# A gated, quantised feed-forward kernel: other orders in its first slots, and its last output tile in two halves

## The chip, the cores and the metric

The kernel runs on one core of a Trainium2 chip. Time is device microseconds of one execution of the whole program; the table below has the runs of the kernel before. The profile is one further execution, recorded by the hardware profiler.

## The reference

Four sequences of 1024 tokens (x is 4 x 1024 x 512) go through a normalised, gated feed-forward layer whose second half is quantised. Cut to what matters:

```python
scale = cond @ norm_w.T + 1.0
ms = jnp.mean(x * x, axis=-1, keepdims=True)
h = x * (scale[:, None, :] * jax.lax.rsqrt(ms + EPS))
u = h @ up_w.T                                  # up_w: 4096 x 512
val, gate = jnp.split(u, 2, axis=-1)
h = val * jax.nn.gelu(gate, approximate=False)  # 2048 wide
hq = act_quant(h)      # per token: round(h * 127 / max|h|), scaled back
wq = weight_quant(down_w)   # round(w / mean|w|) clipped to -1..1, scaled back
y = hq @ wq.T + x                               # down_w: 512 x 2048
```

## The kernel before

The four sequences are the batches b = 0 to 3. The up projection runs in 16 slots j per batch: slot j makes 128 rows of gate and the same 128 rows of value, for all 1024 tokens, which are two halves h of 512 tokens. float32 operands are split into a high and a low float16 part, and the products of high with high, high with low and low with high are summed in PSUM. Batches 1 to 3 multiply with seven combinations of blocks per slot (`slot`, `product`). Batch 0 instead uses plain products (`plain_half`), and beside them it prepares the weights for everybody: weight tile j is loaded (`w_load`), its largest magnitude is found and turned into a power of two (`w_range`), it is scaled (`w_scale`), turned on TensorE into PSUM (`w_turn`), copied as the high part (`w_high`, ScalarE) and subtracted for the low part (`w_low`, VectorE). A float32 copy goes to SBUF (`w_evac`, ScalarE), GpSimd makes sums of its blocks (`s_sums`), and these too are split and spilled to DRAM for the later batches (`s_all`).

The schedule is written out by hand: every engine runs its own instructions in the order of the program text, and an instruction that waits holds up what stands behind it on the same engine. The SP queue issues nearly all DMAs, in the same manner. PSUM has eight banks, given out by tag: "po" has three, "A" and "E" have two each, "B" has one. Each tag goes round its banks in order of allocation, and a new tile waits for the last reader of the tile that had its bank.

The start, lines 695 to 813, is a chain of its own. x's first 512 tokens are four tiles of 128 tokens (`first_load`, one DMA each, L707). ScalarE sums their squares (`first_sum`, L718); `rsqrt_start` makes one over the root (ScalarE L725, VectorE L726 to L730); the tiles are scaled (`first_scale`, L735 on ScalarE, L737 elsewhere), turned on TensorE into four PSUM banks, one for each block k of 128 columns (`first_turn`, L742), and written to SBUF as the high part (`first_high`, ScalarE L746) and the low part (`first_low`, VectorE L750), both with the batch's column scale, which `cond_undo` brings (VectorE L212 to L215). A few matmuls on zeros (`keep_warm`, L758) run in between. W0's gate half (t = 1) goes the same way ahead of its value half. After that `plain_first` runs slot 0's first half (L533), with `second_part` after 6 and `second_slot` after 16 of its matmuls; `plain_half(1, 0, third_slot)` and `plain_half(2, 0, other_half)` follow.

The scale of batches 1 to 3 is a small piece of work beside all this: products and sums (L178, L179), a turn `cond_over` (L192), the largest and its power of two on VectorE (`cond_range`, L198 to L202), and a matmul that spreads it over the partitions (`cond_spread`, L208), which stands in slot 3.

The down projection of a batch runs among the slots of the next one; that of the last batch stands at the end. There its tiles of 128 tokens and 512 columns (four for each half h) take 16 matmuls each (`down_mm`, L684). VectorE multiplies by the token's scale and adds x (`down_end`, L691), and a DMA stores the tile (L692).

Of the kernel before, what the change touches and what calls it, by code (L numbers as in the profile page):

```python
# [17 lines left out]
P = 128  # L18
# [23 lines left out]
def glu_quant_kernel(  # L42
# [15 lines left out]
    HALF = D // 2  # L58
# [180 lines left out]
    def wn(j):  # L239
        return H[:, W_SLOT[j % 3]]  # L240
# [7 lines left out]
    def w_load(j, ts=(1, 0)):  # L248
        for t in ts:
            SP.dma_start(out=wn(j)[:, t], in_=up_v[j][:, t])  # L250

    def w_range(j, t0=0, t1=2):
        t = slice(t0, t1)
        am = sm.tile([P, 2], F32, name=f"wam_{j}_{t0}", tag="wam")[:, t]
        DVE.tensor_reduce(am, wn(j)[:, t], AX.X, ALU.max, apply_absolute_value=True)
        pow2_floor(am)
        DVE.tensor_scalar(sw[:, j, t], am, 2.0**-100, 1.0 / W_UP, ALU.max, ALU.mult)
        if j not in iv:
            iv[j] = sm.tile([P, 2], F32, name=f"iv_{j}", tag="iv", bufs=3)
        DVE.reciprocal(iv[j][:, t], sw[:, j, t])  # L260

    def w_gain(j):
        DVE.tensor_scalar(sg0[:, j, :], sw[:, j, :], dx[:, 0:1], None, ALU.mult)

    def w_scale(j, ts=(1, 0), eng=POOL):
        for t in ts:
            w, r = wn(j)[:, t], iv[j][:, t : t + 1]
            if eng is ACT:
                ACT.activation(w, w, AF.Copy, scale=r)
            else:  # L270
                eng.tensor_scalar(w, w, r, 1.0, ALU.mult, ALU.mult)
# [16 lines left out]
    def w_high(j, ts=(1, 0)):  # L288
        gate, a21, a22 = a_parts(j)
        g, v = (p.rearrange("p (n f) -> p n f", n=2) for p in pw[j])  # L290
        if 1 in ts:
            ACT.copy(gate[:, :, 0], g)
        if 0 in ts:
            ACT.copy(a21[:, 0], v[:, 0])
            ACT.copy(a22[:, 0], v[:, 1])
# [10 lines left out]
    def w_evac(j):  # L306
        for n in range(2):
            ACT.copy(wf(j)[:, 2 * n : 2 * n + 2].rearrange("p n f -> p (n f)"), pw[j][n])  # L308
# [200 lines left out]
        pass  # L509

    def plain_half(j, h, between=nothing):
        pg = bank("A", 2, name=f"pg_{j}_{h}") if h else bank("B", 1, name=f"pg_{j}_{h}")
        plain(j, 1, h, pg)
        t1 = wpool.tile([P, TOK], F32, name=f"g_{j}_{h}", tag="t1")
        ACT.activation(t1, pg, AF.Gelu, scale=gain(j, 1))
        between()
        pv = bank("E", 2, name=f"pv_{j}_{h}")
        plain(j, 0, h, pv)
        DVE.scalar_tensor_tensor(h_half(j, h), pv, gain(j, 0), t1, ALU.mult, ALU.mult)

    def plain_first(between):

        ps = {1: bank("B", 1, name="pg_0_0"), 0: bank("A", 2, name="pv_0_0")}
        gate, a21, a22 = a_parts(0)
        order = [(1, w, 0, k) for k in range(NK) for w in range(2)]
        order += [(0, w, 0, k) for w in range(2) for k in range(NK)]
        order += [(t, 0, 1, k) for t in (1, 0) for k in range(NK)]
        for n, (t, w, l, k) in enumerate(order):
            if n in between:
                between[n]()  # L530
            a = [gate[:, 0], gate[:, 1]] if t else [a21, a22]
            a = a[k // 2].rearrange("p w (k f) -> p w k f", k=2)
            PE.matmul(  # L533
                ps[t], a[:, w, k % 2, :], XP[:, l, k, :TOK],
                start=w + l + k == 0, stop=l == 1 and k == NK - 1,
            )
        t1 = wpool.tile([P, TOK], F32, name="g_0_0", tag="t1")
        ACT.activation(t1, ps[1], AF.Gelu, scale=gain(0, 1))  # L538
        DVE.scalar_tensor_tensor(h_half(0, 0), ps[0], gain(0, 0), t1, ALU.mult, ALU.mult)
# [132 lines left out]
    def rows_of(b, h, a):  # L672
        r = b * S + h * TOK + a * P
        return slice(r, r + P)
# [3 lines left out]
        SP.dma_start(out=xr, in_=xf[rows_of(b, h, a), :])  # L678
        return xr

    def down_mm(b, h, a, po, js):
        q = q_view(b)
        for j in js:
            PE.matmul(  # L684
                po, q[:, h, j, a * P : (a + 1) * P], wd[:, j, :],
                start=j == 0, stop=j == NJ - 1,
            )

    def down_end(b, h, a, po, xr, dq):
        n = h * NA + a  # L690
        DVE.scalar_tensor_tensor(xr, po, dq[:, n : n + 1], xr, ALU.mult, ALU.add)  # L691
        SP.dma_start(out=of[rows_of(b, h, a), :], in_=xr)  # L692


    ctx.enter_context(tc.manual_schedule())
# [10 lines left out]
    def first_load(n, m=1):  # L706
        SP.dma_start(  # L707
            out=X0[:, n : n + m],
            in_=xf[n * P : (n + m) * P, :].rearrange("(s p) d -> p s d", p=P),
        )  # L710
# [21 lines left out]
    def first_scale(n, eng):  # L732
        r = rs0[:, n : n + 1]
        if eng is ACT:
            ACT.activation(X0[:, n], X0[:, n], AF.Copy, scale=r)  # L735
        else:
            eng.tensor_scalar(X0[:, n], X0[:, n], r, 1.0, ALU.mult, ALU.mult)  # L737

    def first_turn(n, pts):
        for k in range(NK):  # L740
            c = (n % NA) * P
            PE.transpose(pts[k][:, c : c + P], X0[:, n, k * P : (k + 1) * P], ident)  # L742

    def first_high(h, k, pt):
        c = slice(h * TOK, (h + 1) * TOK)
        ACT.activation(XP[:, 0, k, c], pt, AF.Copy, scale=scT[:, k, 0:1])  # L746
# [7 lines left out]
    def keep_warm(n):  # L754

        pz = bank("A", 2, name="pz")
        for i in range(n):
            PE.matmul(pz, warm[:, :P], warm, start=True, stop=True)  # L758

    for n in range(NA):  # L760
        first_load(n)
    w_load(0)
    w_load(1)
    first_load(4, 2)
# [9 lines left out]
        first_sum(n)  # L774
    keep_warm(2)
    pd = cond_spread(cond_range(pm, 0, 1), 0, 1, "A")
    keep_warm(5)
    rsqrt_start(ssq0[:, 0:NA], rs0[:, 0:NA])
    for n in (0, 1, 2):
        first_scale(n, ACT)  # L780
    first_scale(3, DVE)
    w_range(0, 1, 2)
    cond_undo(pd, 0, 1)
    w_scale(0, (1,), DVE)
    ptx = [po_bank(f"ptx_0_{k}") for k in range(3)] + [bank("A", 2, name="ptx_0_3")]
    for n in (0, 3, 1):
        first_turn(n, ptx)
    w_turn(0, [bank("E", 2, name=f"pw_0_{t}") for t in (1, 0)], (1,))
    first_turn(2, ptx)
    w_high(0, (1,))  # L790
    first_high(0, 0, ptx[0])
    w_range(0, 0, 1)
    w_low(0, (1,))
    w_scale(0, (0,))
# [10 lines left out]
    def second_part():  # L805
        w_turn(0, ts=(0,))
        w_high(0, (0,))
        w_low(0, (0,))
        w_scale(1, (1,), ACT)
        for k in range(1, NK):  # L810
            first_low(0, k, ptx[k])
        w_evac(0)
        ACT.activation(start_t, neghalf[:, 0:1], AF.Gelu)  # L813


# [77 lines left out]
    def second_slot():  # L893
        w_turn(1)
        w_high(1)
        w_range(2)
        w_gain(2)
        w_scale(2)
        w_low(1)

    def third_slot():
        w_turn(2)
        w_high(2)
        w_evac(2)
        w_low(2)
        first_scale(4, ACT)
        first_scale(5, DVE)
        first_scale(6, ACT)
        first_scale(7, DVE)
# [13 lines left out]

    plain_first({6: second_part, 16: second_slot})
    w_load(3)
    w_evac(1)
    first_sum(4)
    first_sum(5)
# [24 lines left out]
    w_high(3)  # L953
    w_evac(3)
    w_low(3)
    plain_half(1, 1)
    w_load(6)
    for n in D_LOAD[2]:
        d_load(n)
    w_range(5)  # L960
    w_gain(5)
    w_scale(5)
    s_all(2)
    s_sums(3)
# [4 lines left out]
    w_evac(4)  # L969
    w_low(4)  # L970
    plain_half(2, 1)
    pm = cond_over(mx, 1, B, "po")
    dg = cond_range(pm, 1, B)
    s_all(3)
    for n in D_SUM[2]:
        d_sum(n)
# [255 lines left out]
    for h in range(2):  # L1232
        bring_dq = token_undo(b, dq, h, h + 1)
        if h == 0:
            pos = [bank(t, 1 if t == "B" else 2, name=f"po_end_0_{n}") for n, t in enumerate("ABEA")]
        else:
            pos = [po_bank(f"po_end_1_{a}") for a in range(3)] + [bank("E", 2, name="po_end_1_3")]
        cut = NJ - 4
        for j in range(0, cut, 2):
            for a in range(NA):  # L1240
                down_mm(b, h, a, pos[a], (j, j + 1))
            for f in work[:4]:
                f()
            del work[:4]
        for f in work:
            f()
        work = []
        bring_dq()
        for a in range(NA):
            down_mm(b, h, a, pos[a], range(cut, NJ))  # L1250
            down_end(b, h, a, pos[a], XR[:, h * NA + a], dq)
# [1 line left out]
_INS = ["x", "cond_256", "L0_cond_norm_w", "L0_cond_up_w", "L0_cond_down_w"]  # L1253
_OUTS = [((4, 1024, 512), "float32")]
# [23 lines left out]
```

## Time and profile before

| | |
|---|---|
| median of the runs | 750.74 us (750.51 to 751.12, 3 runs) |
| the profiled execution's own time | 748.98 us |
| its span, first to last instruction | 747.0 us |
| TensorE (PE) busy | 737.6 us, 99% |
| VectorE (DVE) busy | 548.7 us, 73% |
| ScalarE (ACT) busy | 376.7 us, 50% |
| GpSimd (POOL) busy | 199.7 us, 27% |
| granted TensorE clock | 1.000 |
| first matmul of slot 0 (L533) | 13.79 us |
| first matmul of slot 1 (L491) | 21.40 us |

Times within the profile are microseconds from the span's start. In the timeline and the chain, a row gives the start, the length, the engine with its line, the operation, the tile written and the tiles read, and how many instructions are merged. In a row of waits, the two times are the total and the longest. A busy matmul in the profile is not the array's own time: matmuls overlap, and back to back those of 512 columns start 0.216 us apart.

### The profile page before, as it was taken

The numbers are of one execution on the slowest core, as the hardware profiler recorded it, in microseconds if no ns is written. First come the engines' busy times: TensorE is split into PE (matmuls) and PEld (weight loads), VectorE is DVE, ScalarE is ACT, GpSimd is POOL, SyncE is SP. The second block draws the span as 40 slices with busy tenths as digits, with TensorE's granted clock in tenths as the row PEclk, the third lists the DMA queues.
The fourth block names the chain that finished last, engine by engine and source line by source line (L and its number), as shares of the span: only waits on it lengthen the run. The fifth ranks groups of instructions, "written<-read, shape, count | busy, mean of one in ns | idle before, by whom it ended". The sixth has DMA issues, their size and how long they took to land.

```text
span 747.0 us, 9574 instructions
## 1 busy us (share of the span) xinstructions
PE 737.6 (99%) x3481; PEld 343.1 (46%) x3481; DVE 548.7 (73%) x794; ACT 376.7 (50%) x617; POOL 199.7 (27%) x219
## 2 busy tenths in 40 slices
PE   7999999999999999999999999999999999999998
PEld 3554545544444444444444444444444444444443
DVE  7868698897989885536689885454778887445896
ACT  6767456565235664534334656453433665332274
POOL 0499487899010030341010030333020000000200
PEclk9999999999999999999999999999999999999999
DMA  7189739777623433765722424466833333233243
GB/s 250 57 321 177 241 108 261 211 180 172 183 86 111 144 107 105 200 209 146 215 99 98 127 77 169 149 196 163 200 103 105 113 112 106 101 99 112 85 156 112
DMA packets 94250, 111.48 MB, mean 149 GB/s; under 512 B 61430, under 2 KB 62071, under 8 KB 94204
## 3 DMA queue, kind: packets, MB, share of 16 engines
q1 hardware_dynamic: 94058, 110.68, 50.4%
q8 instruction: 27, 0.44, 0.2%
q10 hardware_dynamic: 146, 0.20, 0.1%
q14 instruction: 19, 0.16, 0.1%
HBM read 74.66 MB, written 23.09 MB: 131 GB/s over the span
## 4 chain that ended last, share of the span: by engine, by line
PE 96%; DVE 1%; ACT 1%; DMA 1%; issue 0%; SPq 0%; ACTq 0%; DVEq 0%
PE A L476 33%; PE E L476 16%; PE po L684 11%; PE pg L491 11%; PE pv L491 10%; PE B L476 8%; PE po_end L684 4%; PE pw L279 2%; DMA H<-in_x_dram 1%; DVE gm L603 0%; PE ptx L742 0%; PE pg L533 0%; ACT R L718 0%; ACT L813 0%; ACT H L308 0%
## 5 line engine op out<-in xcount | busy, mean ns | idle before, releaser
L476 PEld LDWEIGHTS <-SXY 128*128 128x128 f16 x2016 | 197.1, 98 | 238.2 <-DMA SXY<-s_dram 0.9
L476 PE MATMUL A<-R,SXY 128*128 128x512 f16 x1152 | 264.8, 379 | 0.0
L476 PE MATMUL E<-R,SXY 128*128 128x512 f16 x576 | 140.0, 379 | 0.0
L570 DVE SCALAR_TENSOR_TENSOR H<-A,sg,t 128x512 f32<-128x512 f32 x48 | 36.0, 750 | 80.9 <-PE A L476 80.9
L581 ACT ACTIVATE t<-t,sg 128x512 f32<-128x512 f32 x48 | 34.6, 720 | 106.5 <-DVE t L580 106.5
L684 PE MATMUL po<-wd,R 128*128 128x512 bf16 x384 | 85.3, 379 | 0.0
L684 PEld LDWEIGHTS <-R 128*128 128x128 bf16 x512 | 50.1, 98 | 60.4
L658 DVE TENSOR_TENSOR H<-H,am 128x1024 f32<-128x1024 f32 x64 | 76.2, 1216 | 0.0
L619 POOL PARTITION_ALL_REDUCE am<-R x8 | 14.5, 1818 | 220.6 <-DVE R L605 220.6
L603 DVE TENSOR_REDUCE gm<-H 128x512 f32<-128x1024 f32 x56 | 69.0, 1232 | 2.9 <-DMA wd<-tn 1.9
L476 PE MATMUL B<-R,SXY 128*128 128x512 f16 x288 | 70.0, 379 | 0.0
L580 DVE TENSOR_TENSOR t<-E,t 128x512 f32<-128x512 f32 x48 | 32.6, 679 | 49.4 <-PE E L476 49.4
L385 POOL TENSOR_TENSOR rs<-ssq,neghalf 128x2 f32<-128x2 f32 (+1 forms) x13 | 9.6, 737 | 205.9 <-DVE ssq L384 205.8
L491 PE MATMUL pv<-R 128*128 128x512 f16 x246 | 61.6, 379 | 0.0
L491 PE MATMUL pg<-R,SXY 128*128 128x512 f16 x252 | 57.8, 379 | 0.5 <-ACT g L538 0.5
L491 PEld LDWEIGHTS <-SXY 128*128 128x128 f16 x378 | 37.0, 98 | 42.9 <-issue 0.7
L491 PEld LDWEIGHTS <-R 128*128 128x128 f16 x366 | 35.8, 98 | 41.8
L567 ACT ACTIVATE t<-B,sg 128x512 f32<-128x512 f32 x48 | 33.0, 687 | 37.2 <-PE B L476 37.2
L666 ACT ACTIVATE H<-H 128x1024 f32<-128x1024 f32 x39 | 40.9, 1048 | 20.8 <-DVE H L658 20.8
L551 ACT COPY t<-A 128x512 f32<-128x512 f32 x48 | 28.0, 583 | 45.1 <-PE A L476 44.7
L562 ACT COPY v<-E 128x512 f32<-128x512 f32 x48 | 28.1, 585 | 32.1 <-PE E L476 29.3
L558 ACT COPY B<-A 128x512 f32<-128x512 f32 x48 | 27.4, 571 | 31.0 <-PE A L476 30.2
(154 smaller groups left out, 905.1 us busy)
## 6 DMA issues: line engine op xcount, KB each, us to landing
SXY<-s_dram SPq DMA_DIRECT2D x48, 640.0 KB, 4.1
SXY<-s_dram SPq DMA_DIRECT2D x48, 256.0 KB, 4.5
s_dram<-SXY SPq DMA_DIRECT2D x11, 896.0 KB, 4.0
H<-in_L_cond_up_w_dram SPq DMA_DIRECT2D x32, 256.0 KB, 3.8
xr<-in_x_dram SPq DMA_DIRECT2D x19, 256.0 KB, 5.0
out_dram<-xr SPq DMA_DIRECT2D x19, 256.0 KB, 2.3
s_dram<-R SPq DMA_DIRECT2D x5, 896.0 KB, 12.8
R<-in_L_cond_down_w_dram SPq DMA_DIRECT2D x8, 512.0 KB, 6.0
```

Source lines behind the costliest of these rows:

```text
L476: PE.matmul(o, s[:, w, k, :], tv[:, :, c, l, k, :], start=start and n == 0, stop=stop and n == len(TERMS) - 1, skip_group_check=True,)
L491: PE.matmul(ps, a[k // 2][:, w, k % 2, :], XP[:, l, k, h * TOK : (h + 1) * TOK], start=n == 0, stop=n == len(terms) - 1,)
L551: ACT.copy(cur["t2"], cur["A"])
L562: ACT.copy(cur["v"], cur["E"])
L567: ACT.activation(cur["t1"], pb, AF.Gelu, scale=gain(g, 1))
L570: DVE.scalar_tensor_tensor(h_half(g - 1, 0), prev["A"], gain(g - 1, 0), prev["t1"], ALU.mult, ALU.mult)
L580: DVE.tensor_tensor(prev["t2"], prev["E"], prev["t2"], ALU.add)
L581: ACT.activation(prev["t2"], prev["t2"], AF.Gelu, scale=gain(g - 1, 1))
L603: DVE.tensor_reduce(gm[0], v, AX.X, ALU.max, apply_absolute_value=True)
L658: DVE.tensor_tensor(v, v, r.to_broadcast([P, 2, TOK]), ALU.mult)
L666: ACT.activation(v, v, AF.Copy, bias=MAGIC)
L684: PE.matmul(po, q[:, h, j, a * P : (a + 1) * P], wd[:, j, :], start=j == 0, stop=j == NJ - 1,)
```

## The change

Seven things are changed, and the arithmetic stays as it is:

1. x's first four tiles come in two DMAs of two tiles instead of four of one.
2. `w_range` is cut in two, `w_largest` and `w_factor`. At the start, W0's largest (gate half) stands ahead of the root of x, and the rest of the range stays behind the scalings.
3. Tile 3 of x is scaled by VectorE, 0 and 1 by ScalarE, 2 by GpSimd; W0's gate half is scaled by GpSimd instead of VectorE, ahead of `cond_undo`. TensorE turns the tiles in the order 3, 0, 2, 1 and then W0. The first block's `first_high` stands ahead of `w_high(0)`. Seven warm-up matmuls stand where five did.
4. In `plain_first`, the first four matmuls go through both of the first two blocks with the high part before the low part.
5. In slots 0 to 2: `w_evac(0)` goes from `second_part` (ahead of the table load for GELU) to after `plain_first`; the gate of slot 1's first half gets a bank of tag A instead of B; `w_low(1)` for the gate stands ahead of `w_range(2)`; `w_low(2)` ahead of `w_evac(2)`.
6. `cond_over` and `cond_range` for batches 1 to 3 go from after `plain_half(2, 1)` to before and after `plain_half(1, 1)`.
7. The last tile's 512 columns are done as two halves of 256 in two PSUM banks, the second after everything else; its store is issued from ScalarE's queue.

```diff
+    def w_largest(j, t0=0, t1=2):
         t = slice(t0, t1)
         am = sm.tile([P, 2], F32, name=f"wam_{j}_{t0}", tag="wam")[:, t]
         DVE.tensor_reduce(am, wn(j)[:, t], AX.X, ALU.max, apply_absolute_value=True)
+        return am
+
+    def w_factor(j, am, t0=0, t1=2):
+        t = slice(t0, t1)
         pow2_floor(am)
...
+    def w_range(j, t0=0, t1=2):
+        w_factor(j, w_largest(j, t0, t1), t0, t1)
...
-        pg = bank("A", 2, name=f"pg_{j}_{h}") if h else bank("B", 1, name=f"pg_{j}_{h}")
+        pg = bank(*(("A", 2) if h or j == 1 else ("B", 1)), name=f"pg_{j}_{h}")
...
-        order = [(1, w, 0, k) for k in range(NK) for w in range(2)]
+        order = [(1, w, 0, k) for w in range(2) for k in range(2)]
+        order += [(1, w, 0, k) for k in range(2, NK) for w in range(2)]
...
-    def down_mm(b, h, a, po, js):
+    def down_mm(b, h, a, po, js, c=slice(None)):
...
-                po, q[:, h, j, a * P : (a + 1) * P], wd[:, j, :],
+                po, q[:, h, j, a * P : (a + 1) * P], wd[:, j, c],
...
-        SP.dma_start(out=of[rows_of(b, h, a), :], in_=xr)
+        eng.dma_start(out=of[rows_of(b, h, a), c], in_=xr)
...
-    for n in range(NA):
-        first_load(n)
+    first_load(0, 2)
+    first_load(2, 2)
...
-    keep_warm(5)
+    keep_warm(7)
+    am = w_largest(0, 1, 2)
     rsqrt_start(ssq0[:, 0:NA], rs0[:, 0:NA])
-    for n in (0, 1, 2):
-        first_scale(n, ACT)
-    first_scale(3, DVE)
-    w_range(0, 1, 2)
+    for n, eng in ((3, DVE), (0, ACT), (2, POOL), (1, ACT)):
+        first_scale(n, eng)
+    w_factor(0, am, 1, 2)
+    w_scale(0, (1,))
     cond_undo(pd, 0, 1)
-    w_scale(0, (1,), DVE)
...
-    for n in (0, 3, 1):
+    for n in (3, 0, 2, 1):
         first_turn(n, ptx)
     w_turn(0, [bank("E", 2, name=f"pw_0_{t}") for t in (1, 0)], (1,))
-    first_turn(2, ptx)
+    first_high(0, 0, ptx[0])
     w_high(0, (1,))
-    first_high(0, 0, ptx[0])
...
-        w_evac(0)
         ACT.activation(start_t, neghalf[:, 0:1], AF.Gelu)
...
         w_turn(1)
         w_high(1)
+        w_low(1, (1,))
         w_range(2)
         w_gain(2)
         w_scale(2)
-        w_low(1)
+        w_low(1, (0,))
...
         w_high(2)
+        w_low(2)
         w_evac(2)
-        w_low(2)
...
     w_load(3)
+    w_evac(0)
     w_evac(1)
...
     w_low(3)
+    pm = cond_over(mx, 1, B, "po")
     plain_half(1, 1)
...
     w_gain(5)
+    dg = cond_range(pm, 1, B)
     w_scale(5)
...
     plain_half(2, 1)
-    pm = cond_over(mx, 1, B, "po")
-    dg = cond_range(pm, 1, B)
...
+        cols = [slice(0, D)] * (NA - 1) + [slice(0, HALF if h else D)]
...
-            down_mm(b, h, a, pos[a], range(cut, NJ))
-            down_end(b, h, a, pos[a], XR[:, h * NA + a], dq)
+            c, xr = cols[a], XR[:, h * NA + a]
+            down_mm(b, h, a, pos[a][:, c], range(cut, NJ), c)
+            down_end(b, h, a, pos[a][:, c], xr[:, c], dq, c)
+    c = slice(HALF, D)
+    po = bank("B", 1, name="po_end")[:, c]
+    down_mm(b, h, a, po, range(NJ), c)
+    down_end(b, h, a, po, xr[:, c], dq, c, ACT)
```

More of the change, by code (lines that the diff above doesn't have):

```diff
@@ L250, in w_load @@
             SP.dma_start(out=wn(j)[:, t], in_=up_v[j][:, t])
-    def w_range(j, t0=0, t1=2):
+    def w_largest(j, t0=0, t1=2):
         t = slice(t0, t1)
@@ L684, in down_mm, with down_end @@
             PE.matmul(
-                po, q[:, h, j, a * P : (a + 1) * P], wd[:, j, :],
+                po, q[:, h, j, a * P : (a + 1) * P], wd[:, j, c],
                 start=j == 0, stop=j == NJ - 1,
             )
-    def down_end(b, h, a, po, xr, dq):
+    def down_end(b, h, a, po, xr, dq, c=slice(None), eng=SP):
         n = h * NA + a
         DVE.scalar_tensor_tensor(xr, po, dq[:, n : n + 1], xr, ALU.mult, ALU.add)
-        SP.dma_start(out=of[rows_of(b, h, a), :], in_=xr)
+        eng.dma_start(out=of[rows_of(b, h, a), c], in_=xr)
     ctx.enter_context(tc.manual_schedule())
@@ L1240, in glu_quant_kernel @@
             for a in range(NA):
-                down_mm(b, h, a, pos[a], (j, j + 1))
+                down_mm(b, h, a, pos[a][:, cols[a]], (j, j + 1), cols[a])
             for f in work[:4]:
```

## The prediction

> **What bounds the kernel now.** I read the page first, then TensorE's waits, the start of the chain, and the timelines of three stretches: the first 32 us, 44 to 60 us, and the end.
>
> ```profile
> PE 737.6 (99%) x3481; PEld 343.1 (46%) x3481; DVE 548.7 (73%) x794; ACT 376.7 (50%) x617; POOL 199.7 (27%) x219
> PE 96%; DVE 1%; ACT 1%; DMA 1%; issue 0%; SPq 0%; ACTq 0%; DVEq 0%
> ```
>
> TensorE is busy in 99% of the span and carries 96% of the chain. So only holes in TensorE's row can be won, and a hole is worth its own length. All of TensorE's waits:
>
> ```profile
> PE ptx L742 <- ACT H L735: 1.6, 1, 1.6
> PE pz L758 <- DVE eps L698: 1.4, 1, 1.4
> PE pd L208 <- DVE dg L202: 1.1, 2, 0.6
> PE pg L533 <- ACT R L746: 0.8, 1, 0.8
> PE pg L491 <- ACT g L538: 0.5, 1, 0.5
> PE pw L279 <- DVE H L271: 0.2, 1, 0.2
> ```
>
> The same view from 58 us on is empty. The change can only move the first 58 us and the 3.6 us after the last matmul. The chain of the first stretch (start, length):
>
> ```profile
> 1.77 4.30 DMA H<-in_x_dram
> ...
> 6.10 1.35 ACT R L718 x4
> ...
> 17.27 0.96 ACT H L308 x2
> ...
> 18.24 1.28 ACT L813
> ...
> 20.76 0.60 ACT g L538
> ...
> 21.40 2.75 PE pg L491 x12
> ```
>
> x's second tile lands at 6.07; ScalarE's squares, VectorE's root and the scalings follow; then evacuation (L308), table load (L813) and GELU (L538) hold the matmuls of slot 1 until 21.40.
>
> **The change, part by part.** Two anchors: R is when x's root is ready (9.35 before), W is when w_high(0) has written W0's gate half (13.14 before, L292 at 12.56 + 0.58).
>
> *x in pairs: +0.66.* Before, the squares start at 4.14, 6.10, 6.77 and 7.42; after x1's landing three are left, at a pitch of 0.66. A pair lands whole. If the first pair lands when x1 did, four are left, and R is one square later. The second pair, due when x3 was (7.42 is when SP, waiting for x3, issued again), comes just in time for the third. Bounds: the windows moved 288, 271 and 307 GB/s from 2 to 5 us, so norm_w and two tiles (0.78 MB) could be in by 4.7, and R 0.55 earlier; at worst the pair lands with x3 and R is 2.0 later. I take +0.66, from the row of x1. SP issues two DMAs fewer, so W0's leave 0.96 sooner, but the DMA engines' share is 0.83 to 1.07 from 2 to 13 us: issue is not their limit, nothing.
>
> *W0's largest ahead of the root: 0.* The reduce (0.68) now waits for W0's gate half, and behind it on VectorE stands the root, for which every scaling waits. The half is next in line after x3, one 0.66 later, so about 8.08; the reduce ends at 8.79. ScalarE's square root would end at 9.14. Cover: 0.35; without it the reduce counts in full from there.
>
> *Scalings, turns, W0: W is 0.30 nearer to R.* Before, W = R + 3.79: ScalarE scaled three tiles until R + 1.98, and VectorE scaled W0 at R + 1.99. After: tile 3 (VectorE, 0.49) at R + 0.52, tiles 0 and 1 (ScalarE, pitch 0.62) at R + 0.71 and R + 1.33, tile 2 on GpSimd, which had nothing to do before 13.10. TensorE turns 3, 0, 2, 1 at 0.43 each from R + 0.56, so the last tile's first block is done at R + 2.1; first_high(0) R + 2.13 to 2.76. W0 on GpSimd (0.69 against 0.48) R + 1.4 to 2.1, its turn R + 2.3 to 2.9, w_high then ends at R + 3.48. [...]
>
> ```profile
> 27.77 1.34 DVE L737 TENSOR_SCALAR H<-H,rs 128x512 f32<-128x512 f32 x2
> ...
> 56.30 0.14 DVE L199 TENSOR_SCALAR d<-d 3x1 f32<-3x1 f32 x1
> ...
> 56.65 0.95 DVE L202 TENSOR_SCALAR dg<-ident,d 3x3 f32<-3x3 f32 x1
> ...
> 55.93 2.28 POOL L327 TENSOR_TENSOR SXY<-H,SXY 128x768 f16<-128x768 f32 x2
> ```
>
> Beside GpSimd two scalings take 1.34 instead of 2 x 0.49, and a 3x3 takes 0.95 instead of 0.2; but the 3x1 one takes its 0.14. [...] By the row, one-column operations pass, and only tile 3 and tile 2 exclude each other. VectorE issues next in line, GpSimd 0.09 to 0.12 after a semaphore (13.10 after 12.98), so VectorE should go first: tile 2 is then ready at R + 1.2, before TensorE wants it at R + 1.4. If GpSimd goes first, tile 3 comes at R + 1.1, all turns slip, and W is R + 4.05 (+0.26). I take -0.30.
>
> *From W to slot 1: -0.93.* VectorE goes without a hole from w_low(0) through w_range(1) and the four first_low to 19.42, which is W + 6.28; w_low(0)'s second part waited 0.17 for ScalarE, which is now ahead, so W + 6.13. Before, slot 1's matmuls began at W + 8.26 since GELU stood behind evacuation (1.07) and table load and held bank B. Now evacuation comes after, and the gate half of slot 1 has bank A. The last first_low then decides: matmul of block 3 at W + 6.25, four more of 0.216, slot 1 at W + 7.33. The halved order (both k before the low parts) gives first_high's second block its 0.6 and costs nothing. Evacuation of W0 now ends at W + 8.4 and is wanted at W + 10.7; GELU of slot 1 and w_high(2) come 3.4 and 4.6 after slot 1's start instead of 2.9 and 4.0, wanted at 6.05. w_low(1)'s gate part, put ahead of w_range(2), makes w_scale(2) end 0.3 before its turn: the thinnest cover, priced at what it lacks. Bounds -0.6 (the hole alone) to -1.0.
>
> *The spread of the other batches' scale: -0.74, and a new wait: +0.48.* Before, TensorE's slots end at 56.95 and the spread waits to 57.7 for dg. Moved two slots up, dg is made about 50 us, where VectorE idles 4.7 us: free. But pm takes one of the three "po" banks two turns earlier. w_turn(4) now gets both banks of w_turn(3), not one old bank and the first of them.
>
> ```profile
> 46.01 0.41 DVE L304 TENSOR_TENSOR SXY<-pw,SXY 128x256 f16<-128x256 f32 x1
> ...
> 45.61 1.04 PE L279 MATMUL pw<-ident,H 128*128 128x128 f32 x8
> ```
>
> Their last reader ends at 46.43, the turn's second half began at 46.04: with the semaphore's 0.1, 0.48 late. Both engines hang on the same earlier matmuls, so the lag travels. Bounds: 0 to +0.8. pm itself also waits for mx (40.34, wanted 40.43): a cover of 0.05.
>
> *The last tile in halves: -0.45.*
>
> ```profile
> 742.49 1.61 DVE L691 SCALAR_TENSOR_TENSOR R<-po_end,dq_end,R 128x512 f32<-128x512 f32 x2
> ...
> 743.27 1.20 SPq L692 DMA_DIRECT2D out_dram<-R  x2
> ```
>
> The final operation (0.74) falls to 256 columns, 0.27 less (128x256 against 128x512 from PSUM is 0.41 against 0.69). Its 128 KB, not 256 KB, at some 400 GB/s (the window at 10 us) is up to 0.32 shorter; I take 0.25, as rows of 1 KB appear nowhere. Added: 32 short matmuls for 16, +0.04 at half of 0.216 (if loads don't hide, up to +0.7; but turns pair a 141 ns load with a matmul every 0.108), and ACT's issue 0.37 against 0.33 (ScalarE's own work is over at 736.7, so nothing stands ahead of it). Bounds -0.1 to -0.6.
>
> Sum: +0.66 - 0.30 - 0.93 - 0.74 + 0.48 - 0.45 = **-1.28 us**. The profiled execution took 748.98 (span 747.0 and 1.98 around it), so 747.7; its time is 1.76 below the median of the runs, 750.74, from which the same step gives **749.5**.
>
> **The rivals.** What a measurement of this kernel can tell from no change is about 0.2%, 1.5 us.
>
> *The pair lands by its bytes.* For: x1 came 1.4 us later than the bytes moved would allow, so one late packet may have set 6.07. Against: the squares behind it follow with no room. Then R is between +0.27 (W0's half at 8.08 and its reduce now decide) and -0.55: 748.2 to 749.1.
>
> [...]
>
> [...]
>
> **How the numbers follow.** The sum as it stands 0.45 (its own range 748.6 to 750.2), the early pair 0.25, the port 0.18, the clock or a like loss 0.12. Under 749.24 lie the early pair (0.25) and two fifths of the first case (0.17): 0.42. Over 752.24 lie half of the last case, where the loss of 1.7 meets a pair that lands with x3 (0.06), and a little for what isn't listed: 0.08. The rest, 0.50. The range of eight in ten is 747.9 to 751.2.
>
> **What would show it.** Right: the first square at about 6.1, tile 2 on GpSimd after tile 3 on VectorE, slot 1's matmuls near 20.8, TensorE's wait for GELU gone, a hole of about 0.5 in w_turn(4) near 45, none at the spread, and the last VectorE operation at 0.47. Wrong: squares that start before 5.5, small VectorE operations stretched beside GpSimd, matmuls every 0.43 after 10 us, or any wait of TensorE after 58 us.

## The result, and the profile after

| | before | after |
|---|---|---|
| median of 15 runs each, on the same chip | 750.45 us | 748.08 us |
| lowest to highest | 748.99 to 751.61 | 747.37 to 750.33 |
| the profiled execution | 748.98 (span 747.0) | 747.51 (span 745.7) |

The ratio is 0.9974 (95% interval 0.9965 to 0.9983), which is 1.95 us less (1.3 to 2.6): faster, and by more than the 0.2% that can be told from no change. The profiled pair moved by 1.47 us and its spans by 1.3. The prediction had 1.28 for that pair.

In what follows, line numbers are those of the changed kernel, which stand 7 or 8 higher in the helpers (L742 is now L750). From the page, TensorE's row among the engines, and the chain's shares:

```profile
PE 737.4 (99%) x3481; PEld 344.7 (46%) x3499; DVE 548.7 (74%) x794; ACT 376.5 (50%) x616; POOL 201.6 (27%) x221
PE 98%; DMA 1%; ACT 0%; issue 0%; DVE 0%; SPq 0%
```

TensorE works as long as before (737.6), and its share of the chain rose from 96 to 98%. So what was won are holes and the tail, as the prediction had it. All of TensorE's waits after the change (total, times, longest):

```profile
PE ptx L750 <- DVE wam L136: 1.8, 1, 1.8
PE pz L766 <- DVE eps L706: 1.4, 1, 1.4
PE pg L541 <- ACT SXY L299: 0.7, 1, 0.7
PE pg L541 <- ACT R L754: 0.2, 1, 0.2
```

Three lines of before are gone: the waits for the scale's spread (1.1; of it 0.6 at 57 us, the rest near 7 us, where nothing depended on it), the wait of slot 1 for GELU (0.5), and 0.2 ahead of W0's turn (L279). The first wait names the one-column L136; L136 starts at 10.66, and what the turn needs is tile 3's scaling, which began at 10.26 just ahead of it on VectorE. The chain from the start to slot 1 (start, length):

```profile
1.77 5.89 DMA H<-in_x_dram
...
8.22 0.81 ACT R L726 x3
...
10.26 0.49 DVE H L745
...
10.82 1.95 PE ptx L750 x16
12.76 0.45 PE pw L286 x4
13.24 0.39 ACT SXY L299
...
13.72 0.70 ACT R L754
...
20.35 0.86 PE pv L541 x4
21.21 2.59 PE pg L498 x12
```

The DMA at its head is now the second pair, until 7.66. Evacuation, table load and GELU, which ended the chain of before ahead of slot 1, are not in it any more; TensorE's own matmuls run on from slot 0 into slot 1. A row of the chain begins where the row before it ends; the timelines of ScalarE and TensorE have the starts themselves, of w_high(0) and of slot 1:

```profile
13.24 0.59 ACT L299 CAST SXY<-pw 128x512 f16<-128x512 f32 x1
...
21.05 2.75 PE L498 MATMUL pg<-R,SXY 128*128 128x512 f16 x12
```

The squares on ScalarE and the start of VectorE's and GpSimd's work, from the three engines' timelines:

```profile
5.71 0.63 ACT L726 ACTIVATE R<-H 128x512 f32<-128x512 f32 x1 [2.94 <-DMA H<-in_x_dram]
...
7.68 0.63 ACT L726 ACTIVATE R<-H 128x512 f32<-128x512 f32 x1 [0.64 <-DMA H<-in_x_dram]
```

```profile
8.36 0.69 DVE L255 TENSOR_REDUCE wam<-H 128x1 f32<-128x512 f32 x1 [1.39 <-DMA H<-in_L_cond_up_w_dram]
9.38 0.17 DVE L734 TENSOR_SCALAR ssq<-ssq 128x4 f32<-128x4 f32 x1 [0.34 <-ACT newton L733]
...
10.26 0.49 DVE L745 TENSOR_SCALAR H<-H,rs 128x512 f32<-128x512 f32 x1
10.66 0.15 DVE L136 TENSOR_SCALAR wam<-wam 128x1 int32<-128x1 int32 x1
```

```profile
10.40 0.91 POOL L745 TENSOR_SCALAR H<-H,rs 128x512 f32<-128x512 f32 x1 [9.98 <-DVE rs L738]
```

The third square waits for the second pair. W0's largest (L255) ends 0.34 before the root can start. VectorE's tile goes ahead of GpSimd's, and the one-column operations beside GpSimd keep their 0.15.

The new hole is in w_turn(4), whose eight matmuls now take 1.29 instead of 1.04 in TensorE's timeline and start late as well:

```profile
45.56 1.29 PE L286 MATMUL pw<-ident,H 128*128 128x128 f32 x8
```

The last stores, in the timeline of the end, of VectorE and of the two issuing queues:

```profile
739.97 2.14 SPq L700 DMA_DIRECT2D out_dram<-R  x4
742.62 0.48 DVE L699 SCALAR_TENSOR_TENSOR R<-po_end,dq_end,R 128x256 f32<-128x256 f32 x1 [0.97 <-PE po_end L692]
743.14 0.35 ACTq L700 DMA_DIRECT2D out_dram<-R  x1
```

### The profile page after: what moved, and what is told of

Its sections match the earlier page's. It is cut to its first block, busy times and chain, and to the rows that moved or that the text cites. A ratio compares the mean times of both kernels' runs of the same rounds, so it can differ in the third digit from the quotient of the medians.

```text
span 745.7 us, 9592 instructions
## 1 busy us (share of the span) xinstructions
PE 737.4 (99%) x3481; PEld 344.7 (46%) x3499; DVE 548.7 (74%) x794; ACT 376.5 (50%) x616; POOL 201.6 (27%) x221
## 4 chain that ended last, share of the span: by engine, by line
PE 98%; DMA 1%; ACT 0%; issue 0%; DVE 0%; SPq 0%
PE A L483 33%; PE E L483 17%; PE po L692 11%; PE pg L498 11%; PE pv L498 11%; PE B L483 8%; PE po_end L692 4%; PE pw L286 2%; DMA H<-in_x_dram 1%; PE ptx L750 0%; PE pv L541 0%; PE pg L541 0%; ACT R L726 0%; ACT R L754 0%; SPq L715 0%
## 5 line engine op out<-in xcount | busy, mean ns | idle before, releaser
L692 PE MATMUL po<-wd,R 128*128 128x512 bf16 x369 | 82.4, 379 | 0.8
L692 PEld LDWEIGHTS <-R 128*128 128x128 bf16 x528 | 51.7, 98 | 59.1
L613 DVE TENSOR_TENSOR R<-R,gm 128x512 f32<-128x512 f32 x56 | 42.0, 750 | 1.4
```

The source lines that it names most:

```text
L613: return [largest, lambda: DVE.tensor_tensor(m, m, gm[0], ALU.max)]
L692: PE.matmul(po, q[:, h, j, a * P : (a + 1) * P], wd[:, j, c], start=j == 0, stop=j == NJ - 1,)
```

## The experiments

All are edits of the changed kernel. R and W are the prediction's anchors (x's root ready; w_high(0)'s gate half written). L is when the last of x's first four tiles landed, read from the square that waited for it or from SP's next issue.

**x in single tiles again.**

```diff
-    first_load(0, 2)
-    first_load(2, 2)
+    for n in range(NA):
+        first_load(n)
```

> The changed kernel with x's first four tiles in four loads of one tile again, all else as changed. Theory (a pair lands whole, so the squares start late and bunch up): the first square starts near 4.1 us instead of 5.71, the last ends near 8.2 instead of 9.03. The root on VectorE is then held not by ScalarE but by W0's largest, whose tile lands near 8.1 to 8.3: it starts near 8.8 to 9.05 instead of 9.38, so w_high(0) ends 0.35 to 0.55 earlier than 13.83 and slot 1's first matmul comes near 20.6 instead of 21.05. Rival (the loads' shape is nothing, the late second pair was a chance of the memory): the last square ends near 9.0 again and slot 1 starts at 21.0.

Measured, one run: 747.58 us; R 10.04, W 13.64, slot 1 at 20.86. The absolute times missed the theory, and the rival's too: the last square ended at 8.58, between 8.2 and 9.0, because x's last tile landed at 7.93, not at the 7.40 of before. Against the landing it reads differently. VectorE's first two rows:

```profile
8.61 0.69 DVE L255 TENSOR_REDUCE wam<-H 128x1 f32<-128x512 f32 x1 [1.64 <-DMA H<-in_L_cond_up_w_dram]
9.21 0.16 DVE L734 TENSOR_SCALAR ssq<-ssq 128x4 f32<-128x4 f32 x1
```

The root has no idle time in front of it: here it stands behind W0's largest, which came out 0.17 too late for it. R - L is 2.11, as in the other two profiles with single tiles and the largest in front (2.11 and 2.12, below); it is 1.94 before, and 2.55 or 2.56 in all nine profiles with pairs. So with the landing given, a pair costs about one square (0.62) at R, less the 0.17 by which W0's largest holds up the root of single tiles: 0.45 at W (W - L 6.16 against 5.71). Some 0.1 of that goes again at the other end: from the last matmul's end to the span's end it takes 3.23 or 3.24 in the four profiles with single tiles and the last tile in halves, and 3.11 to 3.15 in the eight with pairs and halves; what makes this difference is open. And L itself came between 7.4 and 8.9 in the fourteen profiles. That is larger than what the shape of the load is worth with the landing given; whether the shape moves L was not settled (last section).

**Single tiles, and W0's largest behind the scalings again.** On top of the edit above:

```diff
-    am = w_largest(0, 1, 2)
     rsqrt_start(ssq0[:, 0:NA], rs0[:, 0:NA])
...
-    w_factor(0, am, 1, 2)
+    w_range(0, 1, 2)
```

> As the last one, and W0's largest (gate half) behind the scalings on VectorE again, as before the change. Theory: nothing but ScalarE's squares sets the root, so it starts near 8.5; W0's scaling on GpSimd comes about 0.7 later from there than in the changed kernel, but TensorE's sixteen turns of x cover that, so w_high(0) ends near 13.0 and slot 1 starts near 20.3, 0.3 earlier than with single loads alone. Rival (W0's largest ahead of the root is what brings W0 in time): w_high(0) ends no earlier than with single loads alone, because W0's turn waits for GpSimd.

Measured, one run: 748.35 us. R 10.56 with L at 8.62: R - L is 1.94, so the wait of the root for W0's largest is gone. But the largest comes back behind tile 3, and GpSimd can scale W0 only later:

```profile
12.35 0.72 POOL L278 TENSOR_SCALAR H<-H,iv 128x512 f32<-128x512 f32 x1 [0.70 <-DVE ux L212]
```

W is R + 3.84 instead of R + 3.60, and W - L is 5.78 against 5.71. The theory that W comes earlier fell; the rival was right. What the move wins behind the root it loses ahead of it when tiles are single. With pairs (the kernel after) it is free, with a cover of 0.34.

**pm in bank B instead of a "po" bank.**

```diff
-        pm = bank(tag, {"po": 3}.get(tag, 2), [B, P], f"pm_{b0}")[: b1 - b0]
+        pm = bank(tag, {"po": 3, "B": 1}.get(tag, 2), [B, P], f"pm_{b0}")[: b1 - b0]
...
-    pm = cond_over(mx, 1, B, "po")
+    pm = cond_over(mx, 1, B, "B")
```

> The changed kernel with the turned maximum of the other batches' scale (pm) in bank B, which stands idle there, instead of one of the three po banks. Theory (pm takes a po bank out of turn, so slot 4's weight turn gets both banks of slot 3's): the hole of TensorE near 45 us, 0.39 in all, is gone, the spread near 57 stays without a wait, and slot 3's gate matmuls (the first after the spread) start 0.35 to 0.45 earlier than 58.38, counted from slot 1's first matmul. Rival (the hole is slot 4's weights or the semaphore's own delay): the hole stays at 0.3 or more.

Measured, one run: 749.29 us. TensorE's timeline at w_turn(4) has no hole:

```profile
46.36 1.03 PE L498 MATMUL pv<-R,SXY 128*128 128x512 f16 x4
47.23 1.04 PE L286 MATMUL pw<-ident,H 128*128 128x128 f32 x8
48.10 1.24 PE L498 MATMUL pg<-R 128*128 128x512 f16 x5
```

From slot 1 to the first gate matmul after the spread it takes 36.88 us instead of 37.33: 0.45 won at this point, so the bank ring made the hole. By the last matmul hardly any of the 0.45 is left. From slot 1 to the last matmul's end it takes 721.45, 721.64 and 721.61 us in the three profiles with pm in bank B (this one and two below), and 721.53 and 721.67 in the two of the kernel after: in those three, later matmuls that wait for stored weight sums lose 0.34, 0.54 and 0.50, in the kernel after none and 0.13. What sets these later holes was not settled. The whole was slower than the kernel after, and two things before slot 1 did that, neither of them near the edit: x's second pair landed at 8.46 instead of 7.66, and TensorE's granted clock fell to half from 12.8 to 16.2 (below); slot 1 came at R + 11.89 instead of R + 10.83.

**The last tile in one piece again.**

```diff
-        cols = [slice(0, D)] * (NA - 1) + [slice(0, HALF if h else D)]
+        cols = [slice(0, D)] * (NA - 1) + [slice(0, D)]
...
-    c = slice(HALF, D)
-    po = bank("B", 1, name="po_end")[:, c]
-    down_mm(b, h, a, po, range(NJ), c)
-    down_end(b, h, a, po, xr[:, c], dq, c, ACT)
```

> The changed kernel with the last tile in one piece of 512 columns, stored from SP, as before. Theory: from the start of the last matmul's row to the end of the span it takes 3.69 us again instead of 3.12, so the time is 0.5 to 0.6 longer, half of it on VectorE (0.74 against 0.48) and half in the store (2.03 from issue to landing against 1.74). Rival (the store's end is a fixed cost, and ScalarE's queue is what was faster): only the 0.26 on VectorE comes back.

Measured, one run: 751.51 us. From the last matmul's end to the span's end it took 3.77 us, against 3.14 in halves and 3.72 in the kernel before: the halves are worth 0.63 there, as the theory had it. The rest of the time went at the start, through the clock again, for twice as long (13.0 to 19.8).

**The same half stored from SP's queue.**

```diff
-    down_end(b, h, a, po, xr[:, c], dq, c, ACT)
+    down_end(b, h, a, po, xr[:, c], dq, c)
```

> The changed kernel with the last half tile's store issued from SP instead of ScalarE's queue. Theory (the gain at the end is the half size: 0.26 on VectorE and 0.3 in the store): from the last matmul's end to the end of the span 3.14 as in the changed kernel, within 0.05. Rival (ScalarE's queue is the faster one): 3.3 or more.

Measured, one run: 747.78 us, and 3.11 us from the last matmul's end to the span's end.

```profile
740.09 3.51 SPq L700 DMA_DIRECT2D out_dram<-R  x5
742.76 0.48 DVE L699 SCALAR_TENSOR_TENSOR R<-po_end,dq_end,R 128x256 f32<-128x256 f32 x1 [0.98 <-PE po_end L692]
```

SP's fifth issue ends 0.36 after VectorE does (743.60 against 743.24), about as ScalarE's does in the kernel after. The half's size made the gain, not the queue.

**The two moves behind slot 1, each undone alone.** Both free slot 1 of GELU: evacuation of W0 goes behind GELU, and the gate of slot 1 gets a bank that GELU doesn't read.

```diff
             first_low(0, k, ptx[k])
+        w_evac(0)
         ACT.activation(start_t, neghalf[:, 0:1], AF.Gelu)
...
-    w_evac(0)
     w_evac(1)
```

> The changed kernel with w_evac(0) ahead of GELU's table load again, and the gate of slot 1 still in bank A. Theory (bank B and the evacuation are one hole together: the matmuls of slot 1 wait for GELU only through bank B): slot 1's first matmul still 7.2 to 7.4 after w_high(0), though GELU comes 1.0 later. Rival (the late table load alone holds slot 1, through w_high(1) and the gate's high part): 7.9 to 8.3.

```diff
-        pg = bank(*(("A", 2) if h or j == 1 else ("B", 1)), name=f"pg_{j}_{h}")
+        pg = bank(*(("A", 2) if h else ("B", 1)), name=f"pg_{j}_{h}")
```

> The changed kernel with the gate of slot 1 in bank B again, and the evacuation left late. Theory: GELU, which ended 7.25 after w_high(0), frees bank B about when the last matmul before is done, so slot 1 starts 7.25 to 7.45 after w_high(0): either of the two moves would have been enough. Rival (bank A is what opens slot 1): 7.7 or more.

Measured, one run each. With evacuation early and bank A, slot 1 began at W + 7.22; with evacuation late and bank B at W + 7.30; with both moves it is W + 7.23, with neither (before) W + 8.25. GELU of slot 0 in ScalarE's timeline, first with evacuation early, then with bank B:

```profile
22.51 0.71 ACT L546 ACTIVATE g<-pg,sg 128x512 f32<-128x512 f32 x1
```

```profile
20.44 0.69 ACT L546 ACTIVATE g<-pg,sg 128x512 f32<-128x512 f32 x1 [0.16 <-PE pg L541]
```

In the first, GELU starts 0.18 before slot 1 (22.69) and slot 1 doesn't care, since it has another bank. In the second, GELU ends at 21.13 and slot 1 follows at 21.18, some 0.07 late. Either move alone is enough to open slot 1, so what they are worth counts once. It is not the whole 1.02, since the kernel before differs in other moves too. Before, slot 0's last matmul would have let slot 1 begin at 20.77 (one step of 0.216 behind it), which is W + 7.63; only the 0.63 from there to 21.40 is the wait for GELU. The other 0.40 is slot 0 itself, whose first matmul comes at W + 0.06 instead of W + 0.64, with the first block's `first_high` ahead of `w_high(0)`; no run takes that part out alone. With both moves undone nothing was run; with evacuation early GELU ends at 23.22, which is W + 7.75, so slot 1 in bank B would have begun near W + 7.8 (an estimate from that row), which is 0.57 late. The times were 749.61 us (early evacuation; the clock fell to half from 12.1 to 15.5, and from slot 1 to the gate matmul after the spread it took 0.39 longer: w_turn(2) begins 0.10 later after slot 1 and takes 1.33 instead of 1.04; what held it is left open) and 747.74 us (bank B).

**More runs, and the number of warm-up matmuls.** The profiles of pm in bank B and of the whole last tile had lost time to the clock at the start, between the warm-up matmuls (L766) and slot 1. The change had raised their number from five to seven. The next four kernels shared a chip and 27 runs of the kernel before (median 750.33): the kernel after as it is, with five, with fourteen, and with fourteen together with single tiles and pm in bank B.

```diff
-    keep_warm(7)
+    keep_warm(5)
```

The kernel after, unchanged:

> The changed kernel unchanged, as the measure for the next three. Theory (two things vary from run to run: the landing of x's last tile, and whether TensorE's granted clock falls to half for a window of 3.4 us after the warm-up matmuls): fastest runs near 747.4 with a mean clock of 1.000, and some runs near 749.5 or later with 0.998 or less. Rival (the spread is measuring noise without a mark in the clock): times at clock 1.000 spread as widely as all.

Five:

> The changed kernel with five warm-up matmuls before the root instead of seven, as before the change. Theory (the warm-up matmuls pay through the clock alone): the fastest runs stay near 747.4, but TensorE idles 0.43 longer, so more runs show a clock of 0.998 or less and the median is 0.5 to 1.5 later than with seven. Rival (they do nothing): median within 0.3.

Fourteen (`keep_warm(14)` in the same line):

> The changed kernel with fourteen of them, so that TensorE works until about 10.4 us and the first turn follows at 10.8 or later. Theory: no run or nearly none with a clock under 0.9995; fastest runs near 747.4 still, the median 0.3 to 1.0 earlier than with seven. Rival (the clock falls for what comes later, the thin stretch from 12.5 to 16 us): as many runs with the lower clock as with seven.

Fourteen, with the edits of the first and the third experiment:

> The changed kernel with three edits: x's tiles in single loads, the turned maximum in bank B, fourteen warm-up matmuls. Theory: 0.45 from the loads (w_high(0) 5.71 after the landing of x's last tile instead of 6.16), 0.45 from the bank (no hole near 45 us), and the clock as with fourteen: fastest runs near 746.5, median 1.2 to 2.0 earlier than the changed kernel's. Rival (gains at the start are taken back, since VectorE and not TensorE paces slots 1 to 3): fastest runs no earlier than 747.0.

And from what these showed, `keep_warm(10)` with the same two edits, beside 13 runs of the kernel before (749.90) on another chip:

> The changed kernel with single loads of x, the turned maximum in bank B, and ten warm-up matmuls instead of fourteen. Theory (fourteen held up the turns: with single loads the root came at 9.56 and w_high(0) 4.22 after it instead of 3.60): w_high(0) within 3.7 of the root, the hole near 45 us gone, nearly no run with a clock under 0.9985, fastest runs near 746.8 and a median 0.5 to 1.0 earlier than the changed kernel's 748.1. Rival (what the start gains, the holes of TensorE later on, where it waits for the stored weight sums, take back): median within 0.3 of the changed kernel's.

| kernel | runs | median, us | lowest to highest | ratio to before (95%) | runs with a mean granted clock of 0.998 or less |
|---|---|---|---|---|---|
| before | 27 | 750.33 | 748.81 to 751.84 | | 13 |
| after (seven) | 10 | 748.18 | 747.37 to 749.88 | 0.9972 (0.9963 to 0.9981) | 1 |
| five | 12 | 750.27 | 747.11 to 752.12 | 0.9991 (0.9977 to 1.0005) | 9 |
| fourteen | 10 | 748.52 | 747.98 to 749.57 | 0.9978 (0.9969 to 0.9987) | 0 |
| fourteen, single tiles, bank B | 6 | 748.32 | 747.82 to 748.98 | 0.9973 (0.9962 to 0.9984) | 0 |
| ten, single tiles, bank B | 9 | 747.90 | 747.71 to 748.16 | 0.9971 (0.9961 to 0.9981) | 0 |

The last column tells which runs lost clock: 3.4 us at half speed (below) take 0.0023 off the mean over 747 us, so one such loss shows as 0.998. One that begins behind the last matmul and is cut short by the end shows as less and costs no matmul time: in the profile of before, the clock is 1.00 from 743.4 to 746.4 and 0.50 from 746.5 to 747.0, the mean is 1.000, and the last matmul ends at 743.32.

Of the expectations, those for the unchanged kernel held (one run of ten lost clock), and with five the median moved by more than the 0.5 to 1.5 expected. With fourteen no run had a mean clock under 0.999, but the median was 0.34 later where 0.3 to 1.0 earlier was expected. With the two other edits the theories fell both times: 1.2 to 2.0 and 0.5 to 1.0 earlier was expected at the median, 0.14 later and 0.2 to 0.3 earlier was measured. The numbers of their rivals came, by which later stages take back what the start gains.

With five the whole change can't be told from no change at the median, although its fastest run is as early as any. Its three runs at full clock have a median of 747.6. So the two warm-up matmuls carry some 2.1 us of the median (750.27 against 748.18), and, as far as these three runs show, through the clock alone. With fourteen no run was at 0.998 or less, but the median wasn't earlier than with seven: the turns came behind more warm-up matmuls (with single tiles W is R + 4.22; with ten it is R + 3.60 again, and so it is in the one profile with fourteen and pairs, where x's last tile landed at 8.81). These profiles also show holes much later, where TensorE waits for stored weight sums. With ten, that is one of the five lines of its waits:

```profile
PE A L483 <- DMA SXY<-s_dram: 0.3, 1, 0.3
```

Such holes, read as the time by which a matmul starts later than 0.216 after the one before it, sum to between 0 and 0.6 us in a profile (before 0.19, after none and 0.13, fourteen 0.56). What sets their size was not settled. The version with ten beats the kernel before. Its median is 0.3 below that of the kernel after, but on another chip and with overlapping ratios, so it can't be told from it; what is plain is that its runs lie within 0.45 us instead of 2.5.

The clock, read by the windows in which it is granted. Each fall to half after the warm-up matmuls lasted about 3.4 us (12.8 to 16.2 with pm in bank B, 12.1 to 15.5 with early evacuation, 12.7 to 16.2 with five) or twice that (13.0 to 19.8 with the last tile whole). Each fence below has, for one profile, the 3.4 us in which TensorE turned x's tiles and, where the clock fell, the one or two such stretches behind it (window, length, TensorE busy and matmuls, its weight loads, VectorE, ScalarE, GpSimd, granted clock, DMA share, GB/s). The kernel after:

```profile
10.30:13.70 3.40, 2.40 (x20) 2.16 (x20) 2.25 (x11) 2.44 (x4) 2.30 (x3) 1.00 0.83 313
```

The kernel after on the shared chip (its profile took 748.89, with the second pair landing at 8.87):

```profile
10.00:13.40 3.40, 1.39 (x13) 1.40 (x14) 2.80 (x14) 1.86 (x5) 1.59 (x2) 1.00 0.98 367
```

With pm in bank B:

```profile
9.40:12.80 3.40, 1.20 (x11) 1.20 (x12) 2.82 (x14) 2.05 (x5) 1.58 (x2) 0.99 1.05 396
12.80:16.20 3.40, 2.72 (x12) 1.99 (x11) 1.13 (x5) 1.79 (x4) 0.70 (x2) 0.50 0.23 75
```

With the last tile whole:

```profile
9.60:13.00 3.40, 1.40 (x13) 1.40 (x14) 2.80 (x14) 1.86 (x5) 1.58 (x2) 1.00 1.02 393
13.00:16.40 3.40, 2.72 (x12) 1.70 (x11) 1.35 (x6) 2.19 (x4) 0.69 (x1) 0.50 0.20 49
16.40:19.80 3.40, 3.40 (x11) 1.67 (x10) 2.35 (x6) 1.32 (x4) 0.69 (x1) 0.50 0.36 120
```

With five warm-up matmuls:

```profile
9.30:12.70 3.40, 0.70 (x6) 0.71 (x7) 2.56 (x14) 2.46 (x7) 1.09 (x2) 1.00 1.06 402
12.70:16.20 3.50, 3.16 (x16) 2.75 (x14) 1.14 (x6) 1.08 (x3) 1.19 (x2) 0.51 0.27 100
```

After 0.70 (five), 0.96 (early evacuation), 1.20 (pm in bank B) and 1.40 us (last tile whole) of matmuls in such a stretch the clock was halved for the next; after 1.39 (the kernel after on the shared chip), 1.68 (SP's store), 1.75 (bank B for the gate) and 2.26 to 2.68 (six more profiles, of before and the kernel after among them) it was not. The edges of the windows are rounded to 0.1 us, and 1.39 and 1.40 lie nearer to each other than that, so these profiles show no amount at which the clock falls. The length of the idle stretch does not sort them: TensorE idled 2.99 us ahead of the turns in the kernel after on the shared chip and kept the clock, and 2.44 with early evacuation and lost it. That more warm-up matmuls help by putting work into this stretch is the author's estimate from these rows; what the runs show is a mean clock of 0.998 or less in 9 of 12 runs with five, 1 of 10 with seven and none with ten or fourteen.

## Why the prediction was right, point by point

The measured median, 748.08, lies in the stated range, 0.2 from its lower end. That the change would be told as faster, under 749.24, had been given 0.42, less than the 0.50 for no difference that can be told. The profiled pair against the steps of the sum:

| step | predicted | measured | how read |
|---|---|---|---|
| R (x in pairs, W0's largest ahead of the root) | +0.66 | +0.88 | 10.22 against 9.34 |
| from R to W | -0.30 | -0.21 | 3.60 against 3.81 |
| from W to slot 1 | -0.93 | -1.02 | 7.23 against 8.25 |
| from slot 1 to the gate matmul after the spread | -0.74 + 0.48 | -0.22 | 37.33 against 37.55 |
| from there to the last matmul's end | +0.04 | -0.17 | 684.20 against 684.37 |
| from there to the span's end | -0.49 | -0.58 | 3.14 against 3.72 |
| sum | -1.28 | -1.32 | spans 745.72 and 747.04 |

Every step went the way that was forecast but one of 0.04, and no step is off by more than 0.22. That the sums agree to 0.04 is partly luck: 0.26 of the first step is a landing that varies by far more between executions, and the -0.17 is a stretch that no edit but the last tile's matmuls touches.

*The pairs.* The price was nearly right by another path. The step "if the first pair lands when x1 did, four are left" failed: the first pair landed 0.36 earlier (first square 5.71, not 6.07), and the second 0.26 later (7.66 against 7.40), so the third square waited 0.64, and two squares behind the second pair set R. Of the +0.88, 0.62 is the shape and 0.26 the later landing. The experiments with single tiles give the price of the shape alone: 0.62 at R for the same landing, 0.45 at W. The rival of an early pair had its early first pair, but it gained nothing, as the second one decides.

*W0's largest.* The cover was 0.34, predicted 0.35; with single tiles it is short by 0.17.

*R to W.* For GpSimd going first the prediction's estimate was R + 4.05. W came at R + 3.60: VectorE's tile went first (10.26 for 0.49, GpSimd's ran from 10.40 for 0.91), and the small operations passed, L136 in 0.15. The records of the two tiles overlap from 10.40 to 10.75, and GpSimd's took 0.91 where W0's scaling of the same size right behind it took 0.71 (L278). The 0.18 that the chances give to "the port" stood for GpSimd going first: no run shows a port, and in this profile VectorE went first. The 0.12 from R + 3.48 to R + 3.60 is small change: TensorE turned without a hole from R + 0.58, but reached W0 at R + 2.38 instead of R + 2.3, and w_high behind it began at R + 3.02.

*W to slot 1.* The wait for GELU is gone, as predicted, and the two single moves show that either is enough; the prediction had one term for both, and they don't add. What then decides was told a little wrong: not the last first_low, but TensorE's own matmuls.

```profile
17.77 2.06 DVE L758 SCALAR_TENSOR_TENSOR R<-ptx,scT,R 128x512 f16<-128x512 f32 x3
...
19.32 1.03 PE L541 MATMUL pg<-R,SXY 128*128 128x512 f16 x4
```

The last first_low ends at 19.83, W + 6.0 (predicted W + 6.13); its matmul is the fourth of the second row and starts at 19.97, right behind the third, so it had 0.14 to spare. TensorE has no idle time from 14.46 on but 0.03 at 16.57, and slot 1 comes at W + 7.23, not W + 7.33.

*The spread and the bank.* At the gate matmul behind w_turn(4) the kernel after is 0.56 later counted from slot 1 (25.64 against 25.08); 0.39 is the hole and 0.17 pm's own turn (L192) with its slot on TensorE, which stood behind this point before. From there to the gate matmul after the spread it wins 0.78. The bank ring was named as the cause and priced at 0.48; moving pm to bank B takes 0.45 back at this point, and later holes take most of it away again.

*The last tile.* -0.45 predicted; the tail gave 0.58 in the profiled pair and 0.63 in the experiment. Its two main terms were near: the store landed 1.74 after its issue against 2.03 (0.29, estimated 0.25), and the last VectorE operation took 0.48 against 0.74 (0.26, estimated 0.27). ScalarE's issue took 0.35 against SP's 0.34, so the 0.04 set against it hardly came.

*The rest.* A hole of 0.2 near 367 us, TensorE waiting for stored sums, is in the profile of before and not in that of after. No edit touches it, and the kernel after on the shared chip has 0.13 of such holes, so this gain is one execution's. The prediction held that nothing between 58 us and the last matmul can move; it had looked at the waits of the matmuls, not at those of their weight loads, and these waited 0.9 for stored sums in the profile of before.

*From the profile to the median.* This is the step that was mis-sized. The prediction took the 1.76 us between the profiled execution and the median for the same in both kernels and came to 749.5. The median fell to 748.08. Of the 1.38 between, 0.29 is the median of before, 750.45 over fifteen runs instead of 750.74 over three; 0.19 is the pair, which moved by 1.47; and 0.90 is this distance, which was 1.47 before and 0.57 after. In the larger set the kernel before has 13 of 27 runs with a granted clock of 0.998 or less, and their median is 750.86 against 749.62 of the others. The kernel after has 5 such runs of 25. At full clock alone the two medians of that set are 749.62 and 748.11: 1.51 apart, close to the pair's 1.47 and to the sum. The medians over all runs of that set are 750.33 and 748.18, 2.15 apart; the remaining 0.64 goes with clock falls that became rarer.

*The clock.* The prediction gave 0.12 to a loss through the clock, as one that the change would add. The clock does fall, to 0.50 from 12.8 to 16.2 with pm in bank B, but it fell in the kernel before already (13 of 27 runs at 0.998 or less), and with the change it was rarer (5 of 25). No run shows the 1.7 that the chances put on such a loss: one fall of 3.4 us cost 1.06 (pm in bank B), 1.28 (early evacuation) and 1.45 (five), and the one of 6.8 us cost 2.34 (last tile whole), read as slot 1 minus R against 10.83. The stretches ahead of a fall were not idle, they held 0.70 to 1.40 us of matmuls. In the profile of before TensorE idled 1.64 us ahead of the first turn (at 10.15) and kept a clock of 1.00; that was one execution, and of 27 about half show a fall. The prediction gave the two added warm-up matmuls no term of their own, and at the median they were worth the most.

## What to carry to other kernels

Where a profile shows one execution, ask which of its waits lie at an edge that moves from run to run, and look at the clock of all the runs before the distance from profile to median is taken for a constant. Cheap matmuls in a stretch where TensorE would idle can be worth more than all the reordering around it (here seven for five moved the median from 750.27 to 748.18, and with five the whole change couldn't be told from none), and they show it in the spread and the median, not in the fastest run. When a tile is moved up in a program with banks given out in turn, follow the ring to its next reader: one transposition in the wrong ring held TensorE for 0.45 us here, in another bank not at all. And follow such a gain to the last instruction: of this one hardly anything was left at the last matmul.

## What the runs showed of the hardware that was not expected

TensorE's clock was halved after stretches of 3.4 us that were not idle: they held 0.70 (five warm-up matmuls), 0.96 (early evacuation), 1.20 (pm in bank B) and 1.40 us (last tile whole) of matmuls. One with 1.39 kept it (the kernel after on the shared chip). In one profile half speed lasted for a second such stretch although TensorE was busy for most of the first: with the last tile whole it held from 13.0 to 19.8, with TensorE 2.72 of 3.40 us busy in the first; with pm in bank B the same 2.72 was followed by full speed (1.00 from 16.4 to 20.0). What tells these two apart was not settled.

x's first four tiles are issued right behind the program's first load, and in fourteen profiles the last of them landed between 7.4 and 8.9 us (7.40, 7.93, 8.62, 7.45 and 8.06 with one; 7.66, 8.46, 8.47, 8.87, 8.86, 8.81, 8.03, 7.72 and 7.69 with two). The means are 7.89 with one and 8.29 with two, which five and nine profiles on several chips don't tell apart. On the shared chip the three with pairs came at 8.8 and the one with single tiles at 7.45, so that pairs land later is a possibility that no run here rules out.
